# First loads on SyncE's queue, weight sums ahead of the last keys, and half a chunk's mix finished on TensorE, in a gated cross-attention kernel

## The chip, the cores and the metric

The kernel runs on one core of a Trainium2 chip. The core has a matrix engine (TensorE, PE in the profile; its weight loads are PEld), a vector engine (VectorE, DVE), an activation engine (ScalarE, ACT), a general engine (GpSimd, POOL) and SyncE (SP), which here only issues DMAs. Each engine works off its own instruction queue in order. DMAs are issued from SP's queue and, at the start and the end, from ACT's queue; a queue that has to wait before it issues a DMA holds back everything behind it on that engine.

The metric is the time of one execution on the device in microseconds (us).

## The reference, cut to what matters

x and ctx are 8 x 512 x 2048 (batch, features, positions) in fp32. Each batch is cut into 16 windows of 128 positions. Attention with 8 heads of 32 runs within each window; queries and keys come from the layer-normalised x (over the 2048 positions), values from ctx. A gated residual follows, then a second layer norm, a router over 64 experts of which the best 8 count, and a second gated residual:

```python
q = einsum('ed,bdw->bew', Wq, qp) + bq[:, None]
k = einsum('ed,bdw->bew', Wk, qp) + bk[:, None]
val = einsum('ed,bdw->bew', Wv, vp) + bv[:, None]
scores = where(mask > 0, einsum('bhdi,bhdj->bhij', qh, kh) / sqrt(32), -1e9)
o = gelu(einsum('bhij,bhdj->bhdi', softmax(scores), vh), approximate=False)
x = x + tanh(g_xattn) * (einsum('de,bew->bdw', Wo, o) + bo[:, None]) * mask
n = layernorm(x)                                   # rows of 2048, 4096 rows in all
scores = softmax(einsum('th,eh->te', n, router_weight) + router_bias)
topk_w, topk_idx = top_k(scores, 8)                # w_dense: these 8, zeros elsewhere
x = x + tanh(g_ffn) * (n * topk_w.sum(-1) + einsum('te,eh->th', w_dense, expert_bias))
```

## The kernel before, in words

**Tiles.** The 512 features are 4 blocks of 128 partitions (m = 0 to 3). A batch's 2048 positions are 4 chunks (ch) of 512; there are 32 chunks in all, and each is handled in two halves of two windows, which are the 64 steps g. Everything is fp32.

**Order.** The order of instructions on every engine is the order in which the program writes them. Tiles come from pools with few buffers, so that an instruction also waits for the reader of the buffer that it is to overwrite. Loads on hardware queues go over eight completion semaphores in turn, so a load is issued only when the load that used its semaphore before has landed.

**The start.** SP and ACT both issue loads: the weights, the first context, all of batch 0's x in 16 pieces of 128 x 512 (`load_first_x(m)`, L148: pieces 0 and 1 of a row block on SP, 2 and 3 on ACT), then the first mask, the bias vectors, the gates and the router bias, all on ACT (L161 to L169). For each row block m, DVE gathers statistics (L260, L243), POOL makes scale and shift (L245 to L251, L273), ACT normalises two chunks (`norm`, L281), and TensorE adds that block's share to the first queries and keys (`first_queries_and_keys`, L336; the results leave through L343 and L348). After the loop DVE makes sums of weight blocks (`weight_sums`, L207 to L209), which the queries and keys of all later chunks use in a form with seven block products instead of eight (`queries_and_keys`, L370), and adds the bias to the first values (`values_out`, L416).

**The steps.** Step g computes scores (L430, L439), maxima (L451, DVE), exponentials (L460, ACT), division (L468, L469), transposes of the attention (`turn`, L483, and its copy L489), and weighs the values of an earlier step (L502). Between these lie the next chunk's queries, keys and values (L370, L407), the output projection with the residual (`attend`, L531, L537, L540), and the transposes of the new x for the router (`turn_x`, L555, copied by ACT at L557). Router logits gather per batch in `lgT` (`logits`, L566). In step 3, `centre_router` subtracts the means from the router weights: a sum on DVE (L732), a small matmul (L734), a subtraction.

**The experts.** While the next batch goes on, `gather` (L590, copied by ACT at L594), `choose` (L601, L605), `choose_exps` (L613) and `select` (L621 to L638) turn the logits of a batch into weights; `turn_weights` (L647, L651) transposes them. `scale_x` (L662 on ACT, L664 on POOL) multiplies x by its factor, `mix` (L677) forms the expert term in eight pieces k of half a chunk, two products each, and `added` adds it on DVE (L687) and issues the store (L691).

**The end.** The last chunk z is written out by hand behind the loop: it has no next chunk to compute, the remaining transposes, projections and statistics of z-1 and z, then the last batch's experts, with the pieces 5, 6 and 7 of the batch before them in between. PSUM banks are taken in turn there (`late`, `product`).

## Time and profile before

| what | us |
|---|---|
| median of 3 runs | 1364.62 |
| lowest, highest | 1362.07, 1364.92 |
| the profiled execution | 1361.84 |
| its span | 1360.0 |
| PE, DVE, ACT, POOL busy | 1305.5, 886.3, 835.7, 791.8 |
| PE busy in the first 34 us | 12.24 |
| PE busy in the last 34 us | 22.26 |

A line of the timeline gives start, duration, engine, line, operation, output <- inputs and a count, and in brackets how long the engine had been idle and what released it. A line of the waits says which engine waited for whom: us in total, times, longest. ACTq and SPq are the queues at the moment they issue a DMA. A matmul in fp32 shows as two records.

### The profile page before, as it was taken

The page shows a single profiled execution, that of the slowest core. Times are in us where ns is not written, and L with a number is a line of the kernel's source. Part 1 is how long each engine was busy: PE and PEld are TensorE (multiplying, and loading weights), DVE is VectorE, ACT ScalarE, POOL GpSimd, SP SyncE. Part 2 cuts the span into 40 slices and gives each one's busy share as a digit, 9 for nine tenths or more (in the row PEclk, how much of TensorE's full clock was granted, in tenths as well). Part 3 has the DMA queues.
Part 4 walks back from the last instruction along what each step waited for, and adds up shares of the span by engine and source line. Part 5 has one row for each costly group of instructions (what it writes and reads, how often), then busy time and mean ns, then how long its engine had stood idle before and what let it go on. Part 6 is the DMA issues. An engine that isn't in the chain of part 4 may idle for free.

```text
span 1360.0 us, 26464 instructions
## 1 busy us (share of the span) xinstructions
PE 1305.5 (96%) x9786; PEld 951.3 (70%) x9786; DVE 886.3 (65%) x1814; ACT 835.7 (61%) x2843; POOL 791.8 (58%) x802
## 2 busy tenths in 40 slices
PE   3899999999999999999999999999999999999996
PEld 2576777777777777776777677777777777776652
DVE  4566656676667766767666766667666665666656
ACT  2374666666567576567667476666656757656652
POOL 3255655566666655667556675556666665566632
PEclk7999999999999999999999999999999999999997
DMA  7532234235344344435344444435534423332124
GB/s 236 132 117 80 83 101 133 80 108 163 125 147 144 94 158 148 147 126 162 99 136 148 135 143 158 124 110 148 164 129 143 148 65 123 132 121 74 63 78 170
DMA packets 109697, 173.32 MB, mean 127 GB/s; under 512 B 9216, under 2 KB 43648, under 8 KB 109440
## 3 DMA queue, kind: packets, MB, share of 16 engines
q1 hardware_dynamic: 105280, 167.53, 38.5%
q10 hardware_dynamic: 4288, 4.10, 0.9%
q8 instruction: 77, 1.26, 0.4%
q14 instruction: 52, 0.43, 0.1%
HBM read 138.06 MB, written 33.55 MB: 126 GB/s over the span
## 4 chain that ended last, share of the span: by engine, by line
PE 89%; DVE 5%; DMA 2%; ACT 2%; POOL 1%; issue 1%; DVEq 0%; ACTq 0%
PE qk L370 27%; PE po L531 17%; PE pv L407 13%; PE pt L483 8%; PE pb L677 5%; PE pa L502 5%; PE pl L566 4%; PE sc L439 4%; PE px L555 3%; PE sc L430 2%; PE pf L336 1%; DMA cx<-in_ctx 1%; POOL at L469 1%; ACT at L460 1%; DVE st L550 1%
## 5 line engine op out<-in xcount | busy, mean ns | idle before, releaser
L469 POOL TENSOR_TENSOR at<-at,rsum 128x1024 f32<-128x1024 f32 x128 | 244.1, 1907 | 312.3 <-DVE rsum L468 295.3
L460 ACT ACTIVATE at<-sc,nmx 128x128 f32<-128x128 f32 x1024 | 364.9, 414 | 12.1 <-DVE nmx L451 12.1
L460 ACT ACTIVATION_READ_ACCUMULATOR at<-sc,nmx 128x1 f32 x1024 | 260.4, 254 | 0.0
L407 PE MATMUL pv<-wv_sb,cx 128*128 128x256 f32 x1024 | 238.6, 381 | 7.3 <-DMA cx<-in_ctx 6.8
L531 PE MATMUL po<-o,wo_sb 128*128 128x512 f32 x512 | 233.7, 599 | 0.2 <-ACT o L525 0.2
L540 POOL TENSOR_TENSOR xr<-t,xr 128x512 f32<-128x512 f32 x124 | 160.5, 1294 | 90.9 <-DVE t L537 90.5
L407 PEld LDWEIGHTS pv<-wv_sb,cx 128*128 128x128 f32 x1024 | 188.6, 191 | 30.1 <-DMA cx<-in_ctx 6.8
L512 ACT COPY o<-pa 128x512 f32<-128x512 f32 x64 | 37.5, 585 | 261.6 <-PE pa L502 261.6
L489 ACT COPY atT<-pt 128x512 f32<-128x512 f32 x256 | 151.0, 622 | 54.1 <-PE pt L483 53.7
L537 DVE SCALAR_TENSOR_TENSOR t<-po,bo_sb,mk 128x512 f32<-128x512 f32 x128 | 96.1, 751 | 109.5 <-PE po L531 109.4
L451 DVE TENSOR_REDUCE nmx<-sc 128x4 f32<-128x512 f32 x256 | 158.8, 682 | 12.3 <-PE sc L439 12.3
L531 PEld LDWEIGHTS po<-o,wo_sb 128*128 128x128 f32 x512 | 94.4, 190 | 100.7 <-issue 93.8
L483 PEld LDWEIGHTS pt<-ident,at 128*128 128x128 f32 x1024 | 122.0, 141 | 54.8 <-issue 37.4
L483 PE MATMUL pt<-ident,at 128*128 128x128 f32 x1024 | 150.2, 275 | 0.3 <-ACT x1T L557 0.2
L557 ACT COPY x1T<-px 128x512 f32<-128x512 f32 x124 | 72.5, 586 | 126.2 <-PE px L555 116.6
L370 PE MATMUL qk<-xt,wq_sb 128*128 128x256 f32 x496 | 128.3, 381 | 3.2 <-DVE u L378 3.2
L370 PE MATMUL qk<-xn,wk_sb 128*128 128x256 f32 x496 | 127.5, 380 | 1.5 <-DVE vT L416 1.5
L370 PE MATMUL qk<-xn,ws 128*128 128x256 f32 x496 | 127.3, 379 | 0.0
L370 PEld LDWEIGHTS qk<-xn,ws 128*128 128x128 f32 x496 | 94.2, 190 | 12.8
L687 DVE TENSOR_TENSOR xr<-pb,xr 128x512 f32<-128x512 f32 x128 | 81.8, 684 | 29.2 <-PE pb L677 26.5
L370 PEld LDWEIGHTS qk<-xn,wk_sb 128*128 128x128 f32 x496 | 89.4, 190 | 11.2 <-issue 1.6
L664 POOL TENSOR_SCALAR xr<-xr,xa,xd 128x512 f32<-128x512 f32 x120 | 94.3, 796 | 0.8
(111 smaller groups left out, 2002.7 us busy)
## 6 DMA issues: line engine op xcount, KB each, us to landing
cx<-in_ctx SPq DMA_DIRECT2D x63, 512.0 KB, 5.3
out_dram<-xr SPq DMA_DIRECT2D x62, 512.0 KB, 3.5
raw<-in_x SPq DMA_DIRECT2D x112, 256.0 KB, 3.4
xn<-in_x SPq DMA_DIRECT2D x28, 1024.0 KB, 7.6
xr<-in_x SPq DMA_DIRECT2D x28, 1024.0 KB, 8.0
mk<-in_mask_Bx1x_ff SPq DMA_DIRECT2D x31, 256.0 KB, 5.6
xr<-in_x SPq DMA_DIRECT2D x8, 256.0 KB, 7.1
xr<-in_x ACTq DMA_DIRECT2D x8, 256.0 KB, 6.0
```

The source lines that it names most:

```text
L370: nc.tensor.matmul(out_, w_[:, j, es], xb[:, j, :], start=(j == 0), stop=(j == NM // 2 - 1))
L407: nc.tensor.matmul(pv[:, i, :], cx[:, m, i * W : (i + 1) * W], wv_sb[:, m, :], start=(m == 0), stop=(m == NM - 1),)
L451: nc.vector.tensor_reduce(p["nmx"][:, r, :, :], p["sc"][r], AX.X, ALU.max, negate=True)
L460: nc.scalar.activation(p["at"][i][:, h, :], p["sc"][r][:, i, e, :], AF.Exp, bias=p["nmx"][:, r, i, e : e + 1], accum_out=p["rsum"][:, i, h ...
L469: (engine or nc.gpsimd).tensor_tensor(p["at"][i], p["at"][i], rs[:, :, None].to_broadcast([P, H, W]), ALU.mult)
L483: nc.tensor.transpose(pt[:, r, :], p["at"][i][:, e * HR + r, :], ident)
L489: nc.scalar.copy(p["atT"][i][:, e * HR : (e + 1) * HR, :], p.pop("pt"))
L531: nc.tensor.matmul(po[:, cs], wo_sb[:, e, m * P : (m + 1) * P], os_[ch][:, e, cs], start=(e == 0), stop=(e == NE - 1),)
L537: nc.vector.scalar_tensor_tensor(t[:, cs], po[:, cs], bo_sb[:, m : m + 1], mks[ch][:, cs], ALU.add, ALU.mult)
L540: (engine or nc.gpsimd).tensor_tensor(xc, t[:, cs], xc, ALU.add)
L664: nc.gpsimd.tensor_scalar(xc, xc, a, d, ALU.mult, ALU.add)
L687: nc.vector.tensor_tensor(xc, pt, xc, ALU.add)
```

## The change

- Of the first x, ACT keeps only the pieces 2 and 3 of the row blocks 0, 1 and 2. The last row block goes on SP, and so do the first mask, the value bias (now first of the small loads), the other bias vectors, the gates and the router bias.
- `weight_sums` and the first two `values_out` stand inside the loop of the start, ahead of the last row block's matmuls, so on DVE ahead of the first keys (L348).
- The sum of the router weights (`router_sums`) is made in step 2, the rest of `centre_router` stays in step 3.
- In step 4 of a batch, `turn_weights` comes before the last `turn_x`, not after it.
- At the end, the four `turn_x` copies of chunk z-2 are made by DVE, not by ACT; piece 5 of the batch before the last comes ahead of the last two `attend`, whose statistics follow both; `gather` leaves the last logits in PSUM and `choose` reads them there.
- Pieces 6 and 7 of the batch before the last (half a chunk in their rows, together one chunk) are formed by `mix_with_x`: TensorE first multiplies x by the identity into the bank and then adds the expert product; ACT copies the sum to x (`mixed_with_x`) and SP stores each quarter of a chunk. Before, DVE added the product to x.
- The stores of the last batch are issued in halves, each behind its own addition.

```diff
@@ -115,9 +115,9 @@
         queue.dma_start(t, rows_of(c, ch // NCH, slice(s0, s0 + HW)))
         cxs[ch, h] = t
 
-    def load_mask(ch, queue=nc.sync):
+    def load_mask(ch):
         t = work.tile([P, CW], F32, tag="mk", name=f"mk_{ch}", bufs=4)
-        queue.dma_start(t, masks[ch // NCH, :, columns(ch)].to_broadcast([P, CW]))
+        nc.sync.dma_start(t, masks[ch // NCH, :, columns(ch)].to_broadcast([P, CW]))
         mks[ch] = t
 
     def load_xr(ch, queue=nc.sync):
@@ -147,7 +147,7 @@
 
     def load_first_x(m):
         for j in range(NCH):
-            queue_ = nc.sync if j < NCH // 2 else nc.scalar
+            queue_ = nc.scalar if j >= NCH // 2 and m < NM - 1 else nc.sync
             queue_.dma_start(xr[j][:, m, :], x[0, m * P : (m + 1) * P, columns(j)])
 
     nc.sync.dma_start(wv_sb, wvT.rearrange("(m p) e -> p m e", p=P))
@@ -158,15 +158,15 @@
     load_cx(0, 1)
     for m in range(1, NM):
         load_first_x(m)
-    load_mask(0, nc.scalar)
+    load_mask(0)
+    nc.sync.dma_start(bv_sb, bv.partition_broadcast(P))
     with nc.allow_non_contiguous_dma(reason="short bias vectors onto partitions"):
-        nc.scalar.dma_start(bq_sb, bq.rearrange("(t p) -> p t", p=P))
-        nc.scalar.dma_start(bk_sb, bk.rearrange("(t p) -> p t", p=P))
-        nc.scalar.dma_start(bo_sb, bo.rearrange("(t p) -> p t", p=P))
-    nc.scalar.dma_start(bv_sb, bv.partition_broadcast(P))
-    nc.scalar.dma_start(gates[:, 0:1], g_xattn.partition_broadcast(P))
-    nc.scalar.dma_start(gates[:, 1:2], g_ffn.partition_broadcast(P))
-    nc.scalar.dma_start(rb_sb, rb.partition_broadcast(P))
+        nc.sync.dma_start(bq_sb, bq.rearrange("(t p) -> p t", p=P))
+        nc.sync.dma_start(bk_sb, bk.rearrange("(t p) -> p t", p=P))
+        nc.sync.dma_start(bo_sb, bo.rearrange("(t p) -> p t", p=P))
+    nc.sync.dma_start(gates[:, 0:1], g_xattn.partition_broadcast(P))
+    nc.sync.dma_start(gates[:, 1:2], g_ffn.partition_broadcast(P))
+    nc.sync.dma_start(rb_sb, rb.partition_broadcast(P))
     load_cx(1, 0)
     load_mask(1)
 
@@ -549,12 +549,15 @@
         st2n[b, m] = n + 1
         nc.vector.bn_stats(st2[b][:, m, n, :], xr[ch][:, m, cs])
 
-    def turn_x(ch, k):
+    def turn_x(ch, k, engine=None):
         px = ps_tr.tile([P, NM, P], F32, tag="tr", name=f"px_{ch}_{k}")
         for m in range(NM):
             nc.tensor.transpose(px[:, m, :], xr[ch][:, m, k * P : (k + 1) * P], ident)
         t = work.tile([P, NM, P], F32, tag="x1T", name=f"x1T_{ch}_{k}", bufs=4)
-        nc.scalar.copy(t, px)
+        if engine is nc.vector:
+            nc.vector.tensor_copy(t, px)
+        else:
+            nc.scalar.copy(t, px)
         x1T[ch, k] = t
 
     def logits(ch):
@@ -582,7 +585,7 @@
 
     experts = {}
 
-    def gather(b):
+    def gather(b, copy=True):
 
         pg = ps_tr.tile([P, NM, E], F32, tag="tr", name=f"pg_{b}")
         t = lgT.pop(b)
@@ -591,15 +594,16 @@
                 pg[:, m, :], t[:, m * P : (m + 1) * P], ident2, start=True, stop=True
             )
         lg = small.tile([P, NM, E], F32, tag="lg", name=f"lg_{b}", bufs=1)
-        nc.scalar.copy(lg, pg)
-        experts.setdefault(b, {})["lg"] = lg
+        if copy:
+            nc.scalar.copy(lg, pg)
+        experts[b].update(lg=lg, pg=lg if copy else pg)
 
     def choose(b):
         t = experts[b]
         lg, rs = t["lg"], t["rs"]
         for m in range(NM):
             nc.vector.scalar_tensor_tensor(
-                lg[:, m, :], lg[:, m, :], rs[:, m : m + 1], rb_sb, ALU.mult, ALU.add
+                lg[:, m, :], t["pg"][:, m, :], rs[:, m : m + 1], rb_sb, ALU.mult, ALU.add
             )
         nm = small.tile([P, NM], F32, tag="nm", name=f"nm_{b}")
         nc.vector.tensor_reduce(nm, lg, AX.X, ALU.max, negate=True)
@@ -682,15 +686,33 @@
     def added(b, k, queues=(nc.sync,)):
         j, mp = k // 2, k % 2
         ch = b * NCH + j
+        n = 2 // len(queues)
         for i, pt in enumerate(held.pop((b, k))):
             xc = xr[ch][:, 2 * mp + i, :]
             nc.vector.tensor_tensor(xc, pt, xc, ALU.add)
-        n = 2 // len(queues)
-        for i, queue_ in enumerate(queues):
-            ms = slice(2 * mp + i * n, 2 * mp + (i + 1) * n)
-            queue_.dma_start(rows_of(out, b, columns(ch))[:, ms, :], xr[ch][:, ms, :])
+            if (i + 1) % n == 0:
+                ms = slice(2 * mp + i + 1 - n, 2 * mp + i + 1)
+                queues[i // n].dma_start(rows_of(out, b, columns(ch))[:, ms, :], xr[ch][:, ms, :])
         if mp == 1:
             del xr[ch]
+
+    def mix_with_x(b, k, i):
+
+        t = experts[b]
+        j, mp = k // 2, k % 2
+        rows = slice(i * E, (i + 1) * E)
+        pt = product([P, CW], f"pb_{b}_{k}_{i}")
+        nc.tensor.matmul(pt, ident, xr[b * NCH + j][:, 2 * mp + i, :], start=True, stop=False)
+        nc.tensor.matmul(
+            pt, t["wT"][rows, mp, :], eb_sb[rows, j * CW : (j + 1) * CW], start=False, stop=True
+        )
+        held[b, k, i] = pt
+
+    def mixed_with_x(b, k, i):
+        j, m = k // 2, 2 * (k % 2) + i
+        ch = b * NCH + j
+        nc.scalar.copy(xr[ch][:, m, :], held.pop((b, k, i)))
+        nc.sync.dma_start(rows_of(out, b, columns(ch))[:, m, :], xr[ch][:, m, :])
 
 
     projections = first_queries_and_keys()
@@ -706,14 +728,14 @@
         norm(1, (m,))
         if m == NM - 1:
             mask(0)
+            weight_sums()
+            values_out(0, 0)
+            values_out(0, 1)
         next(projections)
         if m == 0:
             for i in range(NPP):
                 values(0, 1, i)
     st1.pop(0)
-    weight_sums()
-    values_out(0, 0)
-    values_out(0, 1)
     for k in range(3):
         sums_of_x(1, k)
     weight_sums_in_place()
@@ -727,9 +749,11 @@
     for i in range(2):
         load_raw(*queue.pop(0))
 
+    def router_sums():
+        nc.vector.tensor_reduce(rwsum, rw_sb.rearrange("p k e -> p e k"), AX.X, ALU.add)
+
     def centre_router():
 
-        nc.vector.tensor_reduce(rwsum, rw_sb.rearrange("p k e -> p e k"), AX.X, ALU.add)
         pr = ps_tr.tile([P, E], F32, tag="tr", name="pr")
         nc.tensor.matmul(pr, ones, rwsum, start=True, stop=True)
         nc.vector.tensor_tensor(
@@ -892,9 +916,9 @@
                 values_out(c_, h_)
             if fin == 4:
                 stats()
-            turn_x_(3)
             if fin == 4:
                 turn_weights(b4)
+            turn_x_(3)
             turn_(3)
             if nxt < last and (nxt + 1) % NCH:
                 norm(nxt + 1, (2, 3))
@@ -919,6 +943,8 @@
                 sums_of_x(nxt + 1, 2)
         if g == 1:
             nc.scalar.activation(wo_sb, wo_sb, AF.Copy, scale=tgates[:, 0:1])
+        if g == 2:
+            router_sums()
         if g == 3:
             centre_router()
         read_x(len(pieces))
@@ -966,20 +992,20 @@
     mix(b - 1, 2)
     for k in (4, 5):
         scale_x(b - 1, k)
-    turn_x(z - 2, 0)
+    turn_x(z - 2, 0, nc.vector)
     exps(g, 0)
     values(z, 1, 0)
-    turn_x(z - 2, 1)
+    turn_x(z - 2, 1, nc.vector)
     exps(g, 1)
     divide(g, 0)
     values(z, 1, 1)
     values_out(z, 1)
     turn_(h0, 0, 1)
     exps(g, 2)
-    turn_x(z - 2, 2)
+    turn_x(z - 2, 2, nc.vector)
     mix(b - 1, 3)
     load_xr(z)
-    turn_x(z - 2, 3)
+    turn_x(z - 2, 3, nc.vector)
     exps(g, 3)
     divide(g, 1)
     turn_(h0, 2, 3)
@@ -1021,40 +1047,41 @@
         statistics2(z, m)
     for k in range(KC):
         turn_x(z - 1, k)
+    mix(b - 1, 5)
     for m in (2, 3):
         attend(z, m, engine=nc.vector, tag=t_raw)
+    for m in (2, 3):
         statistics2(z - 1, m)
         statistics2(z, m)
-    aggregated = aggregate(st2.pop(b), NCH, f"2_{b}")
-    experts[b] = dict(zip(("nmean", "rs"), aggregated))
+    experts[b] = dict(zip(("nmean", "rs"), aggregate(st2.pop(b), NCH, f"2_{b}")))
     turn_last(0)
     turn_last(1)
     logits(z - 1)
     logits_out(z - 1)
     turn_last(2)
-    mix(b - 1, 5)
     turn_last(3)
     for k in range(KC):
         x1T[z, k] = xz[:, k, :, :]
     logits(z)
     logits_out(z)
-    gather(b)
-
-    mix(b - 1, 6, hold=True)
+    gather(b, copy=False)
+
+    left = [(b - 1, k, i) for k in (6, 7) for i in range(2)]
+    for x_ in left:
+        mix_with_x(*x_)
     choose(b)
     choose_exps(b)
-    added(b - 1, 6)
-    late[:] = late[-2:] + late[:-2]
-    mix(b - 1, 7, hold=True)
+    for x_ in left[:3]:
+        mixed_with_x(*x_)
     select(b)
     turn_weights(b)
-    added(b - 1, 7)
+    mixed_with_x(*left[3])
     for k in range(2 * NCH):
         scale_x(b, k, (0,), nc.scalar)
         scale_x(b, k, (1,))
     for k in range(2 * NCH):
         mix(b, k, hold=True)
-        added(b, k, (nc.sync, nc.scalar) if k >= 2 * NCH - 2 else (nc.sync,))
+        added(b, k, (nc.sync, nc.scalar if k >= 2 * NCH - 2 else nc.sync))
 
 # ---- launch: one core; inputs and outputs as the reference has them ----
 _TRANSPOSED = ["L0_xattn_Wq", "L0_xattn_Wk", "L0_xattn_Wv", "L0_xattn_Wo", "L0_ffn_router_weight"]
```

## The prediction

> **What bounds the kernel now.** I read the page's busy shares first, then who waits for whom on TensorE in the long middle of the run, then the chain of waits and the timeline at the two ends.
>
> ```profile
> PE 1305.5 (96%) x9786; PEld 951.3 (70%) x9786; DVE 886.3 (65%) x1814; ACT 835.7 (61%) x2843; POOL 791.8 (58%) x802
> PE pb L677 <- ACT wT L651: 2.7, 6, 0.5
> PE sc L430 <- DVE t L537: 2.1, 4, 0.5
> PE sc L430 <- DVE vT L416: 0.6, 1, 0.6
> ```
>
> TensorE (PE) is busy for 96% of the span. The last three lines are all its waits from 130 to 1240 us: 5.4 us of 1110. So the middle is bound by matmul work, and time can be had only at the start, at the end, and in those few waits. The start is where PE is idle most (timeline of the first 50 us):
>
> ```profile
> 6.32 9.27 ACTq L151 DMA_DIRECT2D xr<-in_x  x6
> 13.81 0.19 POOL L273 TENSOR_TENSOR nmr<-nmean,rs 128x1 f32<-128x1 f32 x1
> 24.46 0.44 ACTq L169 DMA_DIRECT2D rb_sb<-in_L_ffn_router_bias  x1
> 24.94 1.28 ACT L281 ACT_TABLE_LOAD   x1 [24.94 <-DMA bk_sb<-in_L_xattn_bk]
> 27.10 3.71 PE L336 MATMUL pf<-xn,wq_sb 128*128 128x512 f32 x4 [14.95 <-ACT xn L281]
> 30.64 1.88 PE L336 MATMUL pf<-xn,wk_sb 128*128 128x512 f32 x4
> 49.87 1.10 PE L370 MATMUL qk<-xn,wk_sb 128*128 128x256 f32 x4 [1.48 <-DVE vT L416]
> 55.62 1.13 PE L370 MATMUL qk<-xt,wq_sb 128*128 128x256 f32 x4 [2.06 <-DVE u L378]
> ```
>
> The scale and shift that ScalarE (ACT) needs to normalise the first quarter of x are ready at 14.0 us. But ACT is still issuing DMAs, each held until an earlier one lands, and its first activation comes after the last issue (24.9) and a table load. PE stands idle for 15 us. That is not a wait for data: it is ACT's own queue.
>
> The clock decides what an early start is worth (stretches: length, PE, PEld, DVE, ACT, POOL, granted clock, DMA share, GB/s):
>
> ```profile
> 12.50:15.00 2.50, 0.00 (x0) 0.00 (x0) 0.00 (x0) 0.00 (x0) 1.15 (x6) 1.00 1.08 374
> 15.00:17.50 2.50, 0.00 (x0) 0.00 (x0) 1.45 (x3) 0.00 (x0) 0.00 (x0) 0.89 1.05 384
> 25.00:30.00 5.00, 2.90 (x4) 1.35 (x5) 1.28 (x4) 4.99 (x7) 2.54 (x11) 0.50 0.09 13
> 112.00:114.00 2.00, 1.86 (x30) 1.74 (x34) 1.22 (x1) 0.00 (x0) 2.00 (x3) 0.63 0.19 73
> ```
>
> **The change, part by part. 1: the first loads.** After it, ACT issues no load past the third row quarter of x; its last issue hung on the landing of wk_sb, 12.6 (issued 2.32, 10.3 to landing). So: table load 13.0 to 14.3 (1.28), first normalisation 14.3 to 15.1 (0.80). PE's queue in order: four matmuls of L336 per row quarter at 0.86 each (two of them, four records, from 30.64 to 32.36), 3.4; values(0,1), 3.4 (32.36 to 35.81); then the other quarters, 3.4 each, not before their shares (21.4, 25.5, 28.3 by the same POOL row) plus 0.8 on ACT: 15.1-18.6, 18.6-22.0, 22.2-25.7, 26.3-29.7, 29.7-33.2. Before, L336 ends at 46.3. **Gain 13.1.**
>
> What SyncE's queue gains is ten issues of 0.33 to 0.52 and two x pieces more. Each is held until the load eight before it has landed. The second row quarter's last SP piece still goes at 15.4, the last quarter's four at 15.8 to 17.0 (two went on ACT at 14 to 15.3). The same bytes run at the same 372 to 388 GB/s, which both queues together reach here; last statistics stay at 25.3, with mask, bq, bk and bv landing by 26 and first read after that (mask 25.6, bq 30.6). Behind them cx(1,0), cx(1,1), the later weights and the first raw pieces are issued from 24 to 30 instead of 18 to 43; 4 MB at 260 to 300 GB/s land by 39, and the first raw piece is read at 44. If one queue were slower than two, this cover is short: the last quarter is 1 MB, 2.8 us at 380 GB/s, 5.5 us at half of that, so 0 to 2.7 lost, of which VectorE's (DVE) queue hides nothing. I take 0, since SP alone moved 398 GB/s in a slice near 39 us. POOL's queue keeps its order.
>
> The idle before PE's new start is 3.0 us (12.15 to 15.15). In the rows above the clock falls at about 16.95 after an idle of 4.8 and at about 112.5 after one of 2.74; an idle of 2.06 at 53.6 left it at 1.00. So the first quarter may run at half speed: 1.7 lost per 3.4, of which 0.9 is slack before the third and fourth quarters. Loss between 0 and 2.5; I take 0, as work resumes before 16.95.
>
> The page "TensorE: Matmul & The Clock Gate" of the Trainium skill, section "HAM oscillation — how this bites in real kernels", speaks against the change: bursts of matmuls with waits between run cold each time, where one late unbroken run pays once. Its Part 1 gives a free-running window of about 3.4 us; the two falls above lie 28 such windows apart, so a phase is visible. By it, with an unlucky phase, the gain of this part would be about 11 (an estimate); by the rows alone it is 13.1.
>
> **2: sums and values in front of the last keys.** The three sums (0.69 each) and two vT (0.65 each) fill DVE from 26.4 to 29.8, when it waits for matmuls (19.11 idle before L348 now). Then keys end at 34.0, scores at 35.3, the qk matmuls follow at once (1.48 saved), and the maxima, which now start at 50.97 behind all this, start at 35.3. From there to the release of PE at 55.62 it is 4.65: 39.9. From 55.62 that is 15.7, so this part brings **2.6**. Bounds 1.5 (the PE wait alone) and 3.4 (DVE's 3.4 of work).
>
> **3: the router's sum one step earlier.** Now `PE pr L734 <- DVE rwsum L732` costs 2.7 and the clock falls behind it: scores at 112.47, the next po at 116.30, 3.8 where 1275.67 to 1277.89 takes 2.2. Afterwards PE waits only for the t of L537 (ends 110.2, plus 0.06): 2.2 and 1.6 saved. Against it, the sum's 1.88 stands in step 2 between vT (91.9) and the raw statistics, where 0.45 is idle: maxima 1.4 later, and PE's wait of 0.29 for u at 98.78 grows by 1.4. **Net 2.4**, bounds 0.3 (no clock gain, all 1.88 paid) and 3.8.
>
> **4: turn_weights before the last turn_x.** Seven batches:
>
> ```profile
> 288.14 0.42 DVE L634 TENSOR_TENSOR rest<-lg,rest 128x256 f32<-128x256 f32 x1
> 288.75 0.57 PEld L555 LDWEIGHTS px<-ident,xr 128*128 128x128 f32 x4
> 290.67 1.13 PE L677 MATMUL pb<-eb_sb,wT 64*128 64x512 f32 x4 [0.45 <-ACT wT L651]
> 1256.98 0.44 PE L647 MATMUL pw<-ident,rest 128*128 128x128 f32 x2 [2.01 <-DVE rest L634]
> ```
>
> In six, rest is done (288.56) before px starts; pw takes its place and wT is copied 0.6 sooner: 0.45 x 6 = **2.7** (0 if DVE takes it back). In the last, with no values to compute, px fills a hole now; afterwards pw waits there and px, pt, pb and the next scores queue behind it: **-0.4** (one px), or -2.1 if the 2.95 idle drops the clock for 3.4.
>
> **5: the end.** x1T copies on DVE free 4 x 0.58 of ACT; pa (1.2 wait for atT, 1301.42) starts 0.6 sooner, as DVE's in-order adds hold the last px bank to 1300.3. Moving mix 5 ahead fills PE's holes before pl(z): 0.3, while the aggregate ends 1.3 later, 1330.8, and its POOL chain (2.7) 0.9 before it is read. The rest:
>
> ```profile
> 1333.76 1.10 PE L590 MATMUL pg<-ident,lgT 128*128 128x64 f32 x8 [0.79 <-DVE lgT L580]
> 1341.05 0.69 PE L647 MATMUL pw<-ident,rest 128*128 128x128 f32 x2 [1.03 <-DVE rest L634]
> 1344.47 1.29 DVE L687 TENSOR_TENSOR xr<-pb,xr 128x512 f32<-128x512 f32 x2 [2.28 <-ACT xr L662]
> 1347.90 7.26 DVE L687 TENSOR_TENSOR xr<-pb,xr 128x512 f32<-128x512 f32 x12 [0.42 <-ACT xr L662]
> 1338.00:1340.00 2.00, 2.00 (x4) 0.45 (x2) 1.64 (x11) 0.23 (x2) 0.09 (x1) 0.50 0.60 228
> ```
>
> From the start of pg, before: pw +7.3, wT read +8.5, first add +10.7 (PE at half clock), last add ends +21.4. After: the logit copy (0.37 and its hand-over, 0.5) goes, rest at +7.2 less 0.5; but PE now has four identity matmuls and four pb, no longer in overlapping pairs, 8 x 0.86 = 6.9, so pw waits until +8.0, and the last scalings and pb behind it. wT +8.9, ACT's copy of the fourth product 0.6, first scaling 0.72: first add +10.3 on a warm clock, then 16 adds at 0.63 without the 0.43 gaps: +20.3. The output goes in halves, so the queue fills sooner. 1.1 here; with 0.6 and 0.3, **2.0**. Bounds -1.5 (2.3 of ACT copies and another 1.2 on PE, all uncovered) and +4 (pw not held back, 1.2, and the output 0.8 sooner).
>
> **Sum:** 13.1 + 2.6 + 2.4 + 2.7 - 0.4 + 2.0 = 22.4. The profiled execution took 1361.84 (span 1360.0, 1.84 around it): 1339.4. The median of the runs, 1364.62, is 2.8 above it: 1342.
>
> **The rivals.** A: the early matmuls stay at half clock through all row quarters. The 17.2 of work then takes 34.4 from 15.1, to 49.5, 3.2 later than now; the other parts keep their 9.3, so a gain near 6: 1358. For it: the 2.74 idle that sufficed; against: the clock was back within 3.5 us of work from 27.1, and gaps after 15.1 are 0.2 and 0.6. Half of it (two cold windows, or x late by 2.7 on one queue) gives 1345 to 1352. B: parts 3 to 5 give nothing, since a new wait (u behind the maxima, pw behind the identity matmuls) takes each place: 15.7 alone, 1349. C, slower: the last row quarter arrives so late on SP that the projections end after 46.3 plus the other parts' 9.3; x would have to land 22.4 after its 22.5, 1 MB in 28 us from its issue, 37 GB/s; at 30 GB/s it is 35 us, and 1372. No row is near: SP's queue alone carries 167 to 398 in the slices after 38 us. D: ACT is not released, its table load held for x up to the last quarter: 22.5 plus 1.3 and 0.8, pf at 24.6 instead of 27.1: 2.5 + 9.3, 1353. The program's waits speak against it: the load waits for one piece of the first quarter (landed 7.8).
>
> **How the numbers follow.** A measurement of this kernel tells 0.2% (2.7 us) from no change. Forecast, 1336 to 1347: 0.62. Partial start, B or D, 1347 to 1354: 0.21. Full A, 1354 to 1361.9: 0.07. Better than 1336: 0.04. No change 0.02, C or anything slower 0.04. The range leaves out what lies above 1354 and below 1336: 0.17.
>
> **What would show it.** ACT's table load near 13 and PE's first pf near 15.1, L336 ending near 33; qk resuming near 40; no wait on rwsum, a longer one on u at step 3; six waits of pb on wT gone; pw at the end waiting for PE itself; granted clock 1.00 from 1338. I am wrong if pf starts early yet ends after 40, or if PE's waits in the middle exceed 10 us.

## The result, and the profile after

The changed kernel takes **1346.16 us** (median of 4 runs, 1344.64 to 1348.75) where the kernel before takes 1364.42 (4 runs beside it, 1362.07 to 1364.92): a ratio of 0.9871, 95% interval 0.9852 to 0.9891. It is faster, by 18.3 us at the medians. The profiled execution took 1346.13 (span 1344.3), which is at the changed kernel's median; the one of before, 1361.84, had been below all four of these. Between the two profiled executions, which is what the sum of the prediction is made on, the gain is 15.7 us and not 22.4.

The busy shares and TensorE's waits from 115 to 1235 us (before has the same three lines of waits in this stretch as from 130 to 1240):

```profile
PE 1307.8 (97%) x9794; PEld 952.0 (71%) x9794; DVE 886.2 (66%) x1814; ACT 837.3 (62%) x2842; POOL 793.5 (59%) x802
```

```profile
PE pl L569 <- DVE xr L692: 3.3, 6, 0.6
PE sc L430 <- DVE t L537: 2.1, 4, 0.5
PE sc L430 <- DVE vT L416: 0.6, 1, 0.6
```

The middle is as full as it was. The six waits of pb for wT (2.7) are gone, and six others, of pl for DVE's additions (3.3), stand where there were none. The timeline of the start (start, duration, engine, line, operation, count, and the idle time before with its releaser):

```profile
6.17 6.84 ACTq L151 DMA_DIRECT2D xr<-in_x  x4
13.10 1.28 ACT L281 ACT_TABLE_LOAD   x1 [13.10 <-DMA wk_sb<-in_L_xattn_Wk]
...
15.26 3.58 PE L336 MATMUL pf<-xn,wq_sb 128*128 128x512 f32 x4 [2.41 <-ACT xn L281]
18.67 1.88 PE L336 MATMUL pf<-xn,wk_sb 128*128 128x512 f32 x4
...
32.43 1.88 PE L336 MATMUL pf<-xn,wk_sb 128*128 128x512 f32 x4
...
41.01 1.13 PE L370 MATMUL qk<-xt,wq_sb 128*128 128x256 f32 x4 [0.95 <-DVE u L378]
```

ACT is done with its loads at 13.0 instead of 24.9, and PE's first pf starts at 15.26 instead of 27.10. But that first group lasts 3.58 where its successors last 1.88. The clock says why (stretches: length, PE, PEld, DVE, ACT, POOL, granted clock, DMA share, GB/s):

```profile
15.00:17.50 2.50, 2.24 (x3) 1.17 (x4) 1.54 (x3) 0.91 (x2) 0.00 (x0) 0.52 1.05 388
17.50:20.00 2.50, 2.50 (x6) 0.95 (x5) 2.47 (x6) 0.00 (x0) 0.92 (x3) 0.80 1.05 386
```

Half clock from 15.09 on, for 3.41 us: the early start ran cold. Last, the last batch's weights and the end:

```profile
1239.46 0.44 PE L651 MATMUL pw<-ident,rest 128*128 128x128 f32 x2 [2.96 <-DVE rest L638]
...
1240.87 2.08 PE L681 MATMUL pb<-eb_sb,wT 64*128 64x512 f32 x4
...
1317.68 1.10 PE L593 MATMUL pg<-ident,lgT 128*128 128x64 f32 x8 [0.79 <-DVE lgT L583]
1318.62 1.08 PE L705 MATMUL pb<-xr,ident 128*128 128x512 f32 x2
1319.63 1.12 PE L706 MATMUL pb<-eb_sb,wT 64*128 64x512 f32 x2
...
1327.01 0.44 PE L651 MATMUL pw<-ident,rest 128*128 128x128 f32 x2
```

pw of the last batch waits 2.96 and the pb behind it takes 2.08, not 1.13: half clock again. At the end the eight identity and expert matmuls go in alternation, about 1.05 each: 8.44 from the first one's weight load (1318.57) to pw (1327.01). pw waits for them, as reckoned, but to 9.33 behind pg, not 8.0.

Below, the *lead* is the start of an instruction on PE in the trace of before less its start in the trace of the run. It shows where time comes and goes. Places are named by the PSUM tile that a matmul writes: pf the first queries and keys, qk the later ones, sc scores, po the output projection, pa the weighed values, pl logits, pg the gathered logits, pw the transposed weights, pb expert products, px and pt transposes.

| place (time before) | changed | what happened |
|---|---|---|
| first pf (27.10) | 11.8 | ACT free earlier |
| qk resumes (55.62) | 14.6 | parts 1 and 2; 15.7 predicted |
| po in step 4 (116.30) | 17.5 | part 3: +3.0 |
| within each of six batches | 17.5, 18.0, 17.5 | part 4: +0.5, given back at pl |
| pa of the last batch (1260.3) | 15.7 | part 4: -1.8, of it 1.6 a fall of the clock |
| pa (1301.42) | 16.3 | x1T copies on DVE: +0.57 |
| pg (1333.76) | 16.1 | mix 5 and the rest: -0.2 |
| end of the span | 15.7 | -0.4 |

### The profile page after: what moved, and what is told of

Read it like the earlier page. It is cut to its first block, busy times and chain, and to the rows that moved or that the text cites. A ratio compares the mean times of both kernels' runs of the same rounds, so it can differ in the third digit from the quotient of the medians.

```text
span 1344.3 us, 26502 instructions
## 1 busy us (share of the span) xinstructions
PE 1307.8 (97%) x9794; PEld 952.0 (71%) x9794; DVE 886.2 (66%) x1814; ACT 837.3 (62%) x2842; POOL 793.5 (59%) x802
## 4 chain that ended last, share of the span: by engine, by line
PE 91%; DVE 6%; ACT 1%; DMA 1%; issue 1%; SPq 0%; DVEq 0%; ACTq 0%
PE qk L370 27%; PE po L531 17%; PE pv L407 15%; PE pt L483 8%; PE pl L569 4%; PE pa L502 4%; PE pb L681 4%; PE sc L439 4%; PE px L555 3%; DVE st L550 2%; PE sc L430 1%; PE pf L336 1%; DVE st L260 1%; DMA wq_sb<-in_L_xattn_Wq 1%; ACT at L460 1%
## 5 line engine op out<-in xcount | busy, mean ns | idle before, releaser
L692 DVE TENSOR_TENSOR xr<-pb,xr 128x512 f32<-128x512 f32 x124 | 79.1, 684 | 30.7 <-PE pb L681 30.7
```

The lines of the kernel that those rows point to most:

```text
L692: nc.vector.tensor_tensor(xc, pt, xc, ALU.add)
```

## The experiments

Each is the changed kernel with one edit (10 has two runs with one edit each, 11 has three edits), and its ratio is to the time of before beside it on the same chip. Beside experiments 1, 6, 8 and 9 before had a median of 1362.81, beside 3, 4, 5 and 7 of 1363.50, beside 2, 10 and 11 of 1361.56. The intervals of most ratios overlap with the changed kernel's, so small effects are read from the leads. A *fall* is a stretch in which the granted clock is 0.50.

### 1. The first loads on both queues again

```diff
-            queue_ = nc.scalar if j >= NCH // 2 and m < NM - 1 else nc.sync
+            queue_ = nc.sync if j < NCH // 2 else nc.scalar
...
-    load_mask(0)
-    nc.sync.dma_start(bv_sb, ...)
+    load_mask(0, nc.scalar)
...
+    nc.scalar.dma_start(bv_sb, ...)     # and the other small loads
```

> The changed kernel with the first loads as before: the last row block's pieces 2 and 3, the mask, the bias vectors, gates and router bias on ACT. Theory (ACT's own queue held the first normalisation): the first pf matmul goes back from 15.3 to about 27.1, L336 ends near 46.3; the order of the sums stays, so qk resumes near 53. Of the 14.6 us that stood at that point 11.5 to 13 are lost: span about 1356, time about 1358. Rival (what came early was paid for by a cold clock and data, and the order of the sums carries the gain): less than 5 us lost, time under 1351.

Measured: 1357.72 (1355.91 to 1359.70), ratio 0.9961 [0.9947, 0.9976]. Its timeline:

```profile
24.87 1.28 ACT L281 ACT_TABLE_LOAD   x1 [24.87 <-DMA bo_sb<-in_L_xattn_bo]
...
27.03 3.78 PE L336 MATMUL pf<-xn,wq_sb 128*128 128x512 f32 x4 [15.67 <-ACT xn L281]
...
54.16 1.13 PE L370 MATMUL qk<-xt,wq_sb 128*128 128x256 f32 x4 [0.94 <-DVE u L378]
```

The table load is back at 24.87, pf at 27.03, and the lead where qk resumes is 1.5 of 14.6. The half clock lasted to 33.05 here (before: to 30.60), which costs this run about 1.2 of its lead. Of the whole change, 11.6 us at the medians hang on which queue issues these loads.

### 2. Two pieces of the last row quarter on ACT

```diff
-            queue_ = nc.scalar if j >= NCH // 2 and m < NM - 1 else nc.sync
+            queue_ = nc.sync if j < NCH // 2 else nc.scalar
```

> The changed kernel with pieces 2 and 3 of the last row quarter of x on ACT again; all small loads stay on SP. Theory (ACT's queue alone held the start: each of its issues waits for an earlier landing): ACT's last issue near 15.3, its table load 15.6, first pf 17.7 instead of 15.3; the last row quarter lands as before and bounds L336, so the lead where the qk matmuls resume is 14.6 to 15.5, at most 1 below that of an execution without a fall (16.1); time 1346 to 1347. Rival (the small loads were not what held it, the x pieces were): pf later than 20 and a lead under 13, time over 1348.

Measured: 1347.72 (1347.51 to 1348.07), ratio 0.9894 [0.9880, 0.9909]. The timeline has the issues, the table load and pf where they were expected:

```profile
5.58 9.70 ACTq L151 DMA_DIRECT2D xr<-in_x  x6
15.37 1.28 ACT L281 ACT_TABLE_LOAD   x1 [15.37 <-DMA xr<-in_x]
...
17.53 3.78 PE L336 MATMUL pf<-xn,wq_sb 128*128 128x512 f32 x4 [5.83 <-DMA xr<-in_x]
...
36.12 1.88 PE L336 MATMUL pf<-xn,wk_sb 128*128 128x512 f32 x4
```

But the lead where qk resumes is 10.9, not 14.6 to 15.5. L336 ends at 38.0, and from 17.53 on PE does not wait: its 17.5 of work (what L336 takes at full clock in experiment 3, 15.12 to 32.64) and 3.0 for a half clock up to 23.62 (from 16.79, twice 3.41) are all there is. So the last row quarter's data does not bound L336, though that was expected; PE's own work does, and the start of pf counts in full. Neither expectation holds whole: pf came when the theory had it, the lead is below the rival's 13. Two issues on ACT cost 2.3 at pf, and a fall of 6.83, twice as long as the changed kernel's, the rest. The time is only 1.6 over the changed kernel's; in the profiled execution that is because the clock did not fall in the last batch (lead 13.83 to 13.60).

### 3. PE kept at work before the first pf

```diff
+    pd = ps_tr.tile([P, 2, DK], F32, tag="tr", name="pd")
+    for i in range(6):
+        nc.tensor.matmul(pd[:, i % 2, :], cxs[0, 0][:, i % NM, 0:W], wv_sb[:, i % NM, :], start=True, stop=True)
     projections = first_queries_and_keys()
```

> The changed kernel with six more matmuls that nothing reads (128 positions of the first context by a block of Wv, into a spare bank) ahead of L336, so that TensorE does not stand idle from 12.1 to 15.3. Theory (the first row quarter ran at half clock because of that idle, 5.1 where 3.4 was reckoned): clock 1.00 from 15 to 20, the first quarter's eight matmuls in 3.4, L336 ends near 33 and not 34.3, and the qk matmuls resume 16.2 ahead of before where the changed kernel had 14.6. If the clock falls by the phase of something else, a fall stays in the first 20 us. If the quarter was long for another reason (x late, ACT late), it stays near 5 at clock 1.00. The time: 1344 to 1346 by the theory; one part in a thousand, so the offset decides and not the median.

Measured: 1344.52 (1342.70 to 1344.68), ratio 0.9861 [0.9846, 0.9876]. In the same stretches as above:

```profile
15.00:17.50 2.50, 2.38 (x6) 1.18 (x7) 1.72 (x3) 0.78 (x2) 0.00 (x0) 1.00 1.05 388
17.50:20.00 2.50, 2.50 (x11) 1.63 (x10) 2.46 (x6) 0.00 (x0) 1.02 (x4) 1.00 1.05 387
```

Full clock, L336 ends at 32.6, and the lead at the resume is 16.1 as expected; the time is not told apart from the changed kernel's. So the first quarter was long for the clock and nothing else, and parts 1 and 2 are worth 16.1 without the fall. The fall does not need curing in every execution: those of three other runs with the unfilled idle (the router's, the pairs' and the next one's) kept the clock too, with leads of 16.0, 16.3 and 13.7.

### 4. The sums and values behind the loop again

```diff
         if m == NM - 1:
             mask(0)
-            weight_sums()
-            values_out(0, 0)
-            values_out(0, 1)
...
     st1.pop(0)
+    weight_sums()
+    values_out(0, 0)
+    values_out(0, 1)
```

> The changed kernel with the weight sums and the first two values back behind the loop of the start, all else as changed. The prediction priced this order at 2.6 (bounds 1.5 to 3.4): the lead where the qk matmuls resume falls from 14.6 to 12.0, time 1348.8. Rival (only PE's wait of 1.48 is worth anything, as undoing the first loads left a lead of 1.5): lead 13.1, time 1347.7. If the clock falls at another place in this execution the lead shifts by up to 1.7, so the waits of PE ahead of L370 decide.

Measured: 1346.99 (1345.29 to 1348.16), ratio 0.9878 [0.9861, 0.9894]. Its timeline:

```profile
15.02 1.98 PE L336 MATMUL pf<-xn,wq_sb 128*128 128x512 f32 x4 [2.68 <-ACT xn L281]
...
41.91 1.13 PE L370 MATMUL qk<-xt,wq_sb 128*128 128x256 f32 x4 [2.06 <-DVE u L378]
```

The clock stayed up here, and the lead is 13.7. Against the 16.0 to 16.3 of the other executions without a fall, the order is worth 2.3 to 2.6; 2.6 was predicted. The medians (1346.99 and 1346.16) do not show it; a fall that comes or stays away is nearly as large. The first loads then carry 16.1 - 2.4 = 13.7 of the two.

### 5. The router's sum in step 3 again

```diff
-        if g == 2:
-            router_sums()
         if g == 3:
+            router_sums()
             centre_router()
```

> The changed kernel with the router's sum back in step 3, directly ahead of the matmul that reads it. Theory (part 3 was worth 3.0 by the leads: the wait of 2.7 and the half clock behind it, less 0.6 of a longer wait on u): the wait on rwsum is back with 2.5 to 2.8, the clock falls behind it between 112 less the lead and two us later, the lead drops by 3 there and the time is near 1349. Rival (the fall is by phase, not by the wait): the wait returns but the clock stays, lead less by 1.5, time 1347.5.

Measured: 1349.47 (1347.28 to 1350.18), ratio 0.9897 [0.9882, 0.9913]. The wait is back, in TensorE's waits from 60 to 118 us:

```profile
PE pr L758 <- DVE rwsum L753: 2.7, 1, 2.7
```

and the clock did not fall behind it:

```profile
94.00:96.00 2.00, 0.00 (x0) 0.00 (x0) 1.97 (x2) 0.00 (x0) 1.75 (x2) 1.00 0.86 327
96.00:98.00 2.00, 1.89 (x50) 1.71 (x54) 1.44 (x2) 0.00 (x0) 2.00 (x3) 1.00 0.03 11
```

With the same wait as before, the lead grows there by 1.6 (16.0 to 17.6): that is the fall alone, which before had. So in the profiled execution the rival holds: the wait need not bring a fall. The median is nearer the theory's 1349, though. The profiled execution was the fastest of four (1347.28 at a mean clock of 0.996; the others 1348.89 to 1350.18 at 0.993 to 0.994), so in the others the clock fell more; where is not known. Part 3's 3.0 is 1.4 of waits (2.7 gone; 0.8 given back at u and behind it in step 2 to 3, 0.4 at a new wait on t) and 1.6 of a clock that fell in the profiled execution of before.

### 6. The weights' transposes behind the last turn_x again

```diff
+            turn_x_(3)
             if fin == 4:
                 turn_weights(b4)
-            turn_x_(3)
```

> turn_weights again behind the last turn_x in all seven batches. Theory from the two traces: in six batches the 0.5 us that pb gains is taken back 4 us later, where the pl matmuls wait for DVE's addition, and in the last batch the 2.96 idle drops the clock and costs 1.8. So the pl waits (3.3 in six) go, the six pb waits (2.7) return, the middle stands where it stood, and the end comes 1.8 earlier: span about 1342.5, time about 1344.4. Rival (my prediction's part 4): 2.7 lost, 0.4 regained, time about 1348.5.

Measured: 1345.75 (1344.26 to 1345.87), ratio 0.9873 [0.9857, 0.9890]. Waits from 115 to 1235, then the last batch:

```profile
PE pb L681 <- ACT wT L655: 2.7, 6, 0.5
```

```profile
1239.40 0.44 PE L651 MATMUL pw<-ident,rest 128*128 128x128 f32 x2 [2.01 <-DVE rest L638]
...
1240.40 2.07 PE L681 MATMUL pb<-eb_sb,wT 64*128 64x512 f32 x4
```

The old waits return, the waits of pl go, and the lead of the middle is the same 17.6: in six batches part 4 is worth nothing. In the last batch the loss did not go away as expected. The idle is 2.01 instead of 2.96, and yet the clock fell and the lead dropped by 1.6. The swap itself costs 0.23: so much was lost in the three executions in which pw came first, waited 2.95 and the clock held (experiments 8 and 2, and the second run of 10).

### 7. The statistics of step 4 behind the mix

```diff
             if fin == 4:
-                stats()
+                stats(False)        # without the four statistics of the new x
...
             mix(mb, k)
+        if fin == 4:
+            for m in range(NM):
+                statistics2(xch, m)
```

> The changed kernel with the four statistics of the new x (DVE) moved in step 4 of a batch from ahead of the weights' transposes to behind the mix; the six batches' new wait was PE at pl L569 on DVE xr L692, 0.55 each. Theory (part 4's 0.5 per batch is real, and is taken back at once because DVE's addition of piece 0, which frees the bank, stands behind the statistics): these six waits go and the lead of the middle grows from 17.5 to about 20.6 by the last batch, time near 1343. Rival (DVE has no slack there, the debt only moves): another wait on DVE, on u, t or vT, takes their place in the same step, the lead stays at 17.5 and the time at 1346.

Measured: 1346.70 (1346.13 to 1347.35), ratio 0.9880 [0.9865, 0.9895]. The six waits of pl are gone, and these stand there, from 115 to 1235:

```profile
PE qk L370 <- DVE lgT L581: 2.3, 6, 0.4
```

The lead stays at 17.9 to 17.7 through the six batches: the rival. Why nothing can be won there, DVE's timeline of the changed kernel shows in one batch:

```profile
271.64 0.69 DVE L416 TENSOR_TENSOR vT<-pv,bv_sb 128x512 f32<-128x512 f32 x1 [0.60 <-PE pv L407]
272.25 2.46 DVE L550 BATCH_NORM_STATS2 st<-xr 128x6 f32<-128x512 f32 x4
274.63 1.27 DVE L260 BATCH_NORM_STATS2 st<-raw 128x6 f32<-128x512 f32 x2
275.82 1.27 DVE L692 TENSOR_TENSOR xr<-pb,xr 128x512 f32<-128x512 f32 x2
277.00 2.47 DVE L451 TENSOR_REDUCE nmx<-sc 128x4 f32<-128x512 f32 x4
279.39 0.68 DVE L581 COPY lgT<-pl 128x512 f32<-128x512 f32 x1
```

From 271.64 to 280.07 DVE has no gap, on an engine that is busy 66% on average. PE needs the additions (for the bank) and the copy of lgT; whichever of them comes last in this row takes back what PE had won.

### 8. Pieces 6 and 7 by DVE again

```diff
-    left = [(b - 1, k, i) for k in (6, 7) for i in range(2)]
-    for x_ in left:
-        mix_with_x(*x_)
+    mix(b - 1, 6, hold=True)
...
+    added(b - 1, 6)
+    late[:] = late[-2:] + late[:-2]
+    mix(b - 1, 7, hold=True)
...
+    added(b - 1, 7)
```

> Pieces 6 and 7 of the batch before the last as before: DVE adds the product to x, no identity matmul; everything else as changed. Prediction's part 5 gave the new form 1.1 us: then 1.1 slower, time about 1347.3. Theory from the trace: the alternation of identity and expert matmuls takes 8.44 us instead of 6.9 and holds pw until 9.3 after pg; without it pw comes at 6.9 after pg, but TensorE idles before and the clock falls, so that the first additions of the last batch run at half the matmul speed again: between 1.0 faster and 0.3 slower, time 1345.2 to 1346.5; granted clock 0.5 from about 20 us before the end.

Measured: 1343.20 (1342.78 to 1344.22), ratio 0.9859 [0.9844, 0.9874]. From pg, pw starts 6.81 later (changed: 9.33; before: 7.29, so leaving the logits in PSUM brought the 0.5 that was reckoned) and the span ends 25.01 later (changed: 26.63). The clock was half for 3.41 from 1323.7, so this end is better by 1.6 even with a fall in it. The rest of the 3.0 at the medians is more than was expected; in the profiled execution it is the fall of the last batch, which did not come (lead 17.5 to 17.3).

### 9. The same four pieces, in pairs

```diff
-    for x_ in left:
-        mix_with_x(*x_)
+    for two in (left[:2], left[2:]):
+        for part in range(2):           # 0: the two identities, 1: the two expert products
+            for x_ in two:
+                mix_with_x(*x_, part)
```

> The same eight matmuls of the pieces 6 and 7 in the order identity, identity, product, product, twice. Theory (what costs is the alternation: a product on 64 rows and an identity on 128 rows don't overlap, two products on the two halves of the rows do): the eight take 4 x 0.86 + 2 x 1.06 = 5.6 to 6.2 us instead of 8.44, pw is then bound by rest at 6.8 after pg, and the end comes 2.0 to 2.4 earlier: span about 1342.1, time about 1344. Rival (each matmul costs 1.05 because it accumulates onto a bank that has just been written): 8.4 as now, no difference.

Measured: 1342.14 (1342.08 to 1343.57), ratio 0.9853 [0.9838, 0.9867]. Its timeline from pg:

```profile
1316.10 1.10 PE L593 MATMUL pg<-ident,lgT 128*128 128x64 f32 x8 [0.80 <-DVE lgT L583]
1317.05 1.94 PE L706 MATMUL pb<-xr,ident 128*128 128x512 f32 x4
1318.91 1.13 PE L710 MATMUL pb<-eb_sb,wT 64*128 64x512 f32 x4
1319.97 1.98 PE L706 MATMUL pb<-xr,ident 128*128 128x512 f32 x4
1321.88 1.13 PE L710 MATMUL pb<-eb_sb,wT 64*128 64x512 f32 x4
1322.94 0.44 PE L651 MATMUL pw<-ident,rest 128*128 128x128 f32 x2
```

The same eight matmuls take 5.9 instead of 8.44: two products, which lie on different halves of the rows, take 1.06 together where one between two identities took 1.05, and an identity takes 0.94. pw starts 0.08 after DVE's rest is ready, 6.84 behind pg, and the end comes 24.3 behind pg, 2.4 sooner than in the changed kernel and 0.7 sooner than with DVE's additions. The 4.0 at the medians is more than that; in the profiled execution the start had no fall either (lead 16.3). The Trainium skill has the mechanism: "TensorE: Matmul & The Clock Gate", Part 3, tells that matmuls which use different row groups of the array run at the same time. The rows agree, if the two products stand next to each other.

### 10. The copies of x1T by ACT again, and piece 5 in its old place

```diff
-    turn_x(z - 2, 0, nc.vector)
+    turn_x(z - 2, 0)                # and 1, 2, 3
```

> The changed kernel with the four copies of the transposed x of chunk z-2 on ACT again. The prediction reckoned 0.6 for them, and the leads showed 0.57 at the third last pa. Theory: the lead at that pa falls by 0.5 to 0.6 against the pa before it and stays so to pg; time 1346.7, not to be told from the changed kernel's by the median. Rival (the 0.57 comes from another edit of the end): the lead does not change there.

Measured: 1346.26 (1345.13 to 1346.74), ratio 0.9881 [0.9864, 0.9897].

```profile
1285.89 1.08 PE L502 MATMUL pa<-atT,vT 128*32 128x128 f32 x32 [1.23 <-ACT atT L489]
```

The wait of pa for atT is back (1.22 before), and the lead stays at 15.53 there instead of growing by 0.57. (With DVE's copies a new wait of 1.0, of pt for x1T, takes back a part.) The other one:

```diff
-    mix(b - 1, 5)
     for m in (2, 3):
         attend(z, m, engine=nc.vector, tag=t_raw)
-    for m in (2, 3):
         statistics2(z - 1, m)
...
     turn_last(2)
+    mix(b - 1, 5)
```

> The changed kernel with piece 5's mix back behind the third turn_last and the statistics again right behind each attend. The prediction reckoned 0.3 for the move. Theory: from the last batch's pa to pg TensorE takes 0.3 longer, the idle ahead of pl(z) returns, time 1346.5. Rival (the hole only moves, as with the weights' transposes in the middle): pg at the same distance behind pa.

Measured: 1344.52 (1344.29 to 1348.26), ratio 0.9877 [0.9860, 0.9894]. In its timeline

```profile
1310.89 1.13 PE L681 MATMUL pb<-eb_sb,wT 64*128 64x512 f32 x4
...
1313.28 1.94 PE L569 MATMUL pl<-xz,rw_sb 128*64 128x512 f32 x8 [0.68 <-ACT xz L1042]
```

pl(z) waits 0.68 for ACT's xz; in the changed kernel it waits 0.72 for the same copy. From the last pa to pg the lead does not change (17.75 to 17.74; in the changed kernel 16.17 to 16.08). Moving piece 5 is worth nothing: the rival. The stores in halves were not undone alone, so what they bring is open.

### 11. Three edits that the others pointed to

```diff
+    # the six unread matmuls of 3 and the pairs of 9, and in step 4:
-            if fin == 4:
+            if not vals:            # the last batch
+                turn_x_(3)
+                pd = ps_tr.tile([P, NM, P], F32, tag="tr", name="pd_")
+                for i in range(5):
+                    nc.tensor.transpose(pd[:, i % NM, :], ident, ident)
+            if fin == 4:
                 turn_weights(b4)
-            turn_x_(3)
+            if vals:
+                turn_x_(3)
```

> Three edits on the changed kernel: the identity and expert matmuls in pairs, six unread matmuls ahead of L336, and in the last batch alone the last turn_x ahead of the weights' transposes with five unread transposes behind it, so that no stretch of 3.41 that the clock can be judged over holds more than 1.95 of idle on TensorE before the end. Theory (every fall of the clock in these runs followed a stretch of 3.41 with 2.02 or more idle, but for one; none followed 1.95 or less): no half clock before 1334 in this execution, lead at the qk resume 16.1, at the last batch's pa near 18.8 where the changed kernel had 15.7, pw at pg + 6.9, span 1338.5 to 1339.5, median 1340 to 1341. Rival (a fall is by chance and not by that count): a fall at 15 or 1239 stays, median as with the pairs alone, 1342.

Measured: **1340.45** (1340.33 to 1341.96), ratio 0.9843 [0.9829, 0.9858]. All its runs are below all of the changed kernel's; from the pairs alone (0.9853) it is not told apart. The start kept its clock (lead 16.1) and pw came 6.85 behind pg. In the last batch the clock fell in spite of the five transposes:

```profile
1238.13 0.51 PE L651 MATMUL pw<-ident,rest 128*128 128x128 f32 x2 [1.41 <-DVE rest L638]
1238.44 1.06 PE L483 MATMUL pt<-ident,at 128*128 128x128 f32 x4
1239.43 2.08 PE L681 MATMUL pb<-eb_sb,wT 64*128 64x512 f32 x4
```

The stretch of 3.41 up to the fall at 1238.36 held 1.70 of idle, which by the expectation was safe. So that count is not the whole rule (below), and the lead at pa was 17.5, not 18.8. The profiled execution was the slowest of the four: the other three are 1.5 shorter, at a mean clock of 0.998 and not 0.996, so there this fall may be missing.

## Why the prediction was right, and where not

**The direction and the bulk were right, for the reason given**: ACT's queue of loads, not the data, held PE's start. Table load 13.10 (predicted near 13), pf 15.26 (15.1), no wait on rwsum, a longer wait on u at step 3 (0.29 to 0.89), the six waits of pb gone, pw at the end waiting for PE, the clock at 1.00 behind pg until PE is done: all as announced. The median lies 0.8 inside the upper end of the forecast's 1336 to 1347. Rival D (table load held) and C (SP too slow for the last quarter) did not occur: the last statistics ended at 23.8 (before 25.3), and from 18.1, when ACT's last load had landed, to 22 SP alone moved 375 to 391 GB/s. The sum by its terms:

| term | predicted | measured | |
|---|---|---|---|
| 1 and 2, first loads, sums ahead | 15.7 | 14.6 | 16.0 to 16.3 without a fall; order 2.4 of it |
| 3, router's sum | 2.4 | 3.0 | 1.4 where before's clock does not fall |
| 4, six batches | 2.7 | 0.0 | DVE takes it back |
| 4, last batch | -0.4 | -1.8 | -0.23 without the fall |
| 5, x1T | 0.6 | 0.57 | |
| 5, mix 5 | 0.3 | -0.1 | nothing; -0.2 with the rest up to pg |
| 5, from pg to the end | 1.1 | -0.4 | alternation: 8.44, not 6.9 |
| sum | 22.4 | 15.7 | 14.6 - 0.1 (steps 1, 2) + 3.0 - 1.8 + 0.57 - 0.2 - 0.4 = 15.7 |

**"Loss between 0 and 2.5; I take 0, as work resumes before 16.95"** failed. 16.95 was where the clock fell in the profiled execution of before; in the changed kernel's it fell at 15.09, and the first quarter took 5.1 instead of 3.4. L336 ended at 34.3 instead of 33.2, and the lead is 1.4 to 1.7 below that of executions without a fall. The bound was right and the choice of its end was not: the place of a fall belongs to the execution. This is a sliver of rival A. Its reason, half clock through all row quarters, did not hold: the clock was back at 18.50, after 3.41 us.

**"0.45 x 6 = 2.7 (0 if DVE takes it back)"** failed at its bound, and the second half of rival B was right for it, with another waiter than I named (not pw, but pl and the bank that DVE's addition frees). The prediction read PE's row, where rest is done early; the row of DVE behind it has no gap for 8.4 us.

**"-0.4 (one px), or -2.1 if the 2.95 idle drops the clock"**: the second value came, 1.8. The end chosen was the one that the row did not support: an idle of 2.74 had sufficed at 112.5, and 2.95 is longer. But it is not the idle's length alone: without a fall the swap cost 0.23.

**"8 x 0.86 = 6.9"** is the term that was mis-sized at the end: 8.44, 1.05 each. The price was that of like matmuls in a row. With it, pw at pg + 8.0 became pg + 9.33, the first add +11.5 where +10.3 was reckoned, and 1.1 became -0.4. The order of the eight, not the move to TensorE, cost it: in pairs the same work makes the end 2.4 shorter than in the changed kernel.

**1342 against 1346.2**: the sum was 6.7 too large (22.4 for 15.7), which alone would have given 1339.4. The 2.8 that were added, because before's profiled execution lay below its median, brought the forecast nearer, and that was luck: the changed kernel's profiled execution lay at its median, so the allowance stood for nothing there.

## What to carry to other kernels

A queue that issues loads delays the first instruction behind them by as long as its last issue is held: move loads from an engine that has work to one that has none (here the table load came at 13.10 and not at 24.87), and count what the early work is then worth at the clock that it gets. Before a wait is booked as gain, read the row of the engine that released it for the next 8 us: where that has no gap, the wait moves and the time stays. Matmuls on different halves of the rows belong next to each other: two took 1.06 together here, and 1.05 each when mixed one by one with full ones.

## What the runs showed of the hardware

**The clock changed only at points that lie whole multiples of 3.413 us apart.** The falls of one execution lie whole multiples apart: 16.95, 112.53, 1337.91 and 1354.98 in before are 28, 387 and 392 times 3.413 after the first, and the half clock lasts one or more whole stretches. Where the grid lies differs from execution to execution. I counted for each such stretch at full clock how long neither a matmul nor a weight load ran (from 9 us on, in the 14 profiled executions of before, the changed kernel and the experiments). With 2.02 us or more idle, 33 of 33 were followed by half clock. With 1.3 to 1.98, 3 of 18 were (1.43, 1.49 and 1.70), and 15 were not, the longest with 1.98. So in these executions an idle need not fill a stretch: 2.02 within one was enough each time, while one of 2.7 that is cut by the grid (1.87 in one stretch, in experiment 5) did nothing. The three falls at less idle are behind stretches with transposes or with matmuls on half the rows; the clock may count these for less than the profile books, but no run here shows that, and it stays open. Each fall of 3.41 cost 1.4 to 1.7 where PE was full behind it. The Trainium skill, "TensorE: Matmul & The Clock Gate", Part 1, has the free-running window of 3.4 us, with which the multiples agree, and gives an idle window as the condition of a fall; here 60% of one sufficed.

**One kernel, two falls that come and go.** With an unfilled idle of 2.4 to 3.6 before the first pf, the clock fell in some executions and not in others; with the wait of 2.96 in the last batch likewise. The four timed runs of the changed kernel fit this: 1344.64, 1346.13, 1346.20 and 1348.75 had a mean granted clock of 0.997, 0.996, 0.996 and 0.993, and one fall more is 0.0013 of the mean clock and up to 1.7 us (estimates from 3.41 of half clock in 1345). So falls account for most of the spread of 4.1 us, as far as three digits of the clock tell, and small edits had to be judged by leads between falls and not by medians.
